# Two transformer layers on one core: copies of transposed chunks by ScalarE alone, or by whichever of VectorE and ScalarE is free

## The chip, the cores and the metric

The kernel runs on 1 core of one Trainium2 chip. A core has TensorE (PE in the profile, its weight loads PEld), VectorE (DVE), ScalarE (ACT), GpSimd (POOL) and SyncE (SP), each with its own queue of instructions that it works through in order, and DMA queues that move data between HBM and the on-chip memory SBUF. Matmul results land in PSUM, a small memory that VectorE and ScalarE read. The metric is the device time of one execution in microseconds (us).

## The reference

Input x is 2 x 1024 tokens of width 512, all in fp32. Two layers follow each other, each of two parts, and every part ends in `x = layernorm(x + part(x))`:

```
q, k, v = silu(x Wq), silu(x Wk), silu(x Wv)              # 16 heads of 32
S_t = exp(ld) S_(t-1) + k_t v_t^T ;  o_t = q_t S_t         # linear attention with decay
o = rmsnorm_per_head(o * sigmoid((x Wg1) Wg2)) * w ; part = o Wo
part = fwht(silu(x W1^T) * (x W3^T)) W2^T                  # fwht: Hadamard transform over 2048
dt_r, B, C = split(x Wbc^T) ; delta = softplus(dt_r Wdt^T + b_dt)
h_t = exp(delta_t A) h_(t-1) + (delta_t x_t) B_t ; part = sum_n h_t[n] C_t[n] + x D   # scan, 32 states
part = (silu(x Wg^T) * (x Wu^T)) Wd^T
```

The first two lines with S are layer 0's attention, then layer 0's feed-forward net; the scan is layer 1's mixer, and the last line layer 1's net.

## The kernel before

**Tiling.** Tokens are cut into chunks of 128 (the partitions of SBUF) and chunks into five groups, `GROUPS`: group 0 has the first 2 chunks of sequence 0, group 1 the first 4 of sequence 1, group 2 the next 4 of sequence 0, group 3 the last 4 of sequence 1, group 4 the last 2 of sequence 0. A chunk of x lies as tokens x 512 columns in a tile `xn`. A matmul over the 512 columns needs them on the partitions, so the chunk is transposed first.

**Phases.** Each group passes through `V` (values of the attention, L607), `A` (the rest of the attention, `L658` its projections of q and k, L845 scores, L891 and L900 outputs, L1003 the product with Wo), `F` (layer 0's net: L1052 gate and up products, L1106 the product with Wd), the scan, and `f` (layer 1's net, same lines). `PHASES` gives the order in which phases take PE: V0 A0 V1 A1 F0 F1 V2 A2 f0 F2 V3 A3 a1 F3 V4 A4 b1 F4 f2 f3 f4. Here a1 and b1 are the two halves of f1. F0, f0, a1 and b1 are fillers: they run at a lower priority in the gaps of the attention of another group, and read the tile `xf` instead of `xT`.

**Turning a chunk.** `turn(dst, gi, c, stage)` transposes chunk c of group gi four times 128x128 on PE (L527) into one PSUM bank of the pool `mm` (four banks), and a small thread `copied` copies the bank into its columns of the tile `xT` or `xf` (L534). It is called for every chunk four times: stage 0 for V, 1 after the attention for F, 2 for the scan's inputs, 3 after the scan for f. That makes 64 copies of 128x512, all on ScalarE.

**The scan's inputs.** `Scan.inputs` turns the group's chunks (stage 2), starts `residual` for each (L1284 on POOL), multiplies all of them by Wbc (L1252, which needs the last copy), copies the result (L1258, ScalarE), and multiplies by Wdt (L1269); four softplus chains on ScalarE (L1303 to L1313) and products on POOL (L1322, L1330) follow. The scan itself is POOL's products (L1390), ScalarE's exponentials (L1410), VectorE's scans (L1438) and products (L1451), and sums on POOL and by accumulating DMAs (L1487, L299); VectorE's last column of a unit is kept by ScalarE (L1463). `outputs` transposes the sums back on PE (L1516), and VectorE adds them to the chunk (L1531).

**Normalization.** `normalized` is three small instructions on VectorE (L556 to L558) and four on ScalarE (L562 to L565) for each chunk. ScalarE uses several tables of functions; a change of table is an ACT_TABLE_LOAD.

**The order.** All work is written as generators that yield `Op`s. The class `Order` runs them against its own model of the five engines before anything is built: `free[engine]` is the time at which the model has the engine free, `begin` when an op's operands and buffers are there, `us` its modelled duration. For each engine the best op is taken: of those that could start when the engine becomes free, the one of the lowest `prio` (and, after that, the one that needs no other table), otherwise the one that can start first; among the engines the one whose op starts earliest goes next. The order in which ops are put is the order of each engine's queue on the chip, where semaphores make an instruction wait for its operands. A copy of a transposed chunk has prio -1, a normalization between parts -2, scans and their products 1. The model's constants are in the class (`HOP`, `QUEUE`, and so on).

The pool `mm` holds 4 PSUM banks for nearly all of PE's results. VectorE has one other stream before the first scan: the Hadamard transform of W2 (butterflies L1167, then products L1186 on PE).

Of the kernel before, what the change touches and what calls it, by code (L numbers as in the profile page):

```python
# [53 lines left out]
class Buf:  # L54


    def __init__(self, refs=1):
        self.t = None
        self.written = None
        self.last = 0.0  # L60
        self.refs = refs
# [6 lines left out]
class Op:  # L68

    def __init__(self, eng, us, fn, r=(), w=(), a=(), free=(), prio=0, table=None, dma=0,
                 spare=0):
        self.eng, self.us, self.fn, self.prio, self.table, self.dma = eng, us, fn, prio, table, dma
        self.r, self.w, self.a, self.free, self.spare = r, w, a, free, spare


class Order:
# [4 lines left out]


    ENGINES = ("PE", "DVE", "ACT", "POOL", "SP")
    HOP = 0.08
    QUEUE = 220e3
    FIRST, ALONE = 350e3, 30.0

    def __init__(self):
        self.free = {e: 0.0 for e in self.ENGINES}
        self.queue = {e: 0.0 for e in self.ENGINES}
        self.tags = {}
# [8 lines left out]
    def spawn(self, gen, prio=0):  # L103
        self.new.append([gen, prio, None])

    def begin(self, op, spare=True):

        t = self.free[op.eng]
        for b in op.r:
            if b.written is None:  # L110
                return None
            t = max(t, b.written + self.HOP)
        for b in op.w:
            t = max(t, b.last + self.HOP)
        for name in {name for name, _ in op.a}:
            n, _, bufs = self.tags[name]
            k = sum(name == v for v, _ in op.a) + (op.spare if spare else 0) - (n - len(bufs))
            if k > 0:
                free = sorted(b.last for b in bufs if b.refs <= 0)
                if len(free) < k:  # L120
                    return None
                t = max(t, free[k - 1] + self.HOP)
        return t
# [42 lines left out]
    def run(self):  # L166
        while True:
            while self.new:
                th = self.new.pop(0)
                if self.advance(th):  # L170
                    self.threads.append(th)
            best = {}
            last = None
            moved = False
            for th in list(self.threads):
                op = th[2]
                if not isinstance(op, Op):
                    if op():
                        moved = True
                        if not self.advance(th):  # L180
                            self.threads.remove(th)
                    continue
                t = self.begin(op)
                if op.spare:
                    t0 = self.begin(op, False)
                    if t0 is not None and (last is None or t0 < last[1]):
                        last = None, t0, th
                if t is None:
                    continue
                prio = op.prio + th[1]  # L190
                wrong = self.switches(op)
                now = t <= self.free[op.eng]
                key = (0, prio, wrong, t) if now else (1, t, prio, wrong)
                if op.eng not in best or key < best[op.eng][0]:
                    best[op.eng] = (key, t, th)
            if moved or self.new:
                continue

            if last and ("PE" not in best or best["PE"][1] > last[1] + 1.0):
                best["PE"] = last  # L200
            if not best:
                assert not self.threads, [
                    (th[0].__name__, getattr(th[2], "eng", None)) for th in self.threads
                ]
                return
            _, t, th = min(best.values(), key=lambda v: v[1])
            self.put(th[2], t)
            if not self.advance(th):
                self.threads.remove(th)
# [3 lines left out]
def two_layers(  # L213
# [5 lines left out]
    nc = tc.nc  # L219
# [63 lines left out]
    def pe(us, fn, **kw):  # L283
        return Op("PE", us, fn, **kw)
# [235 lines left out]
    def turn(dst, gi, c, stage, prio=-1):  # L520

        bank = Buf()
        at = dst.cs.index(c)

        def transposes():
            for db in range(EB):
                nc.tensor.transpose(  # L527
                    bank.t[:, db * P : (db + 1) * P],
                    xn[gi, c].t[:, db * P : (db + 1) * P], ident,
                )  # L530

        def copied():
            yield Op(
                "ACT", 0.68, lambda: nc.scalar.copy(  # L534
                    dst.t[:, :, at * P : (at + 1) * P],
                    bank.t.rearrange("p (k t) -> p k t", t=P),
                ),
                r=[bank, dst.whole], w=[dst.parts[at]], free=[bank], prio=-1,
            )

        yield pe(0.62, transposes, r=[xn[gi, c], there[gi, c, stage], ident_b],
                 a=[("mm", bank)] + ([] if at else [(dst.tag, dst.whole)]), prio=prio)
        spawn(copied())
# [1114 lines left out]
```

## Time and profile before

| | us |
|---|---|
| median of 3 runs | 1821.92 (1817.36 to 1825.52) |
| profiled execution | 1821.05 |
| its span | 1819.3 |
| PE busy | 1769.7 |
| VectorE busy | 1283.0 |
| ScalarE busy | 1160.8 |
| GpSimd busy | 1097.2 |
| mean granted TensorE clock | 0.987 |

The times of the profile are of one execution, counted from the start of its span. Lines of an instruction read: start, duration, engine, line, operation, output <- input, shape, how many, and in brackets how long the engine was idle before it and whose end released it. Several instructions of a kind in a row are merged into one line. Lines of waits read: who waited <- for whom, us in total, times, the longest. `ACT_TABLE_LOAD` is a change of ScalarE's table. fp32 matmuls of the program show as two in the profile, so that a product over the 512 columns is eight.

Around the 64 copies, from the groups of instructions: 56 into `xT` take 586 ns each and 8 into `xf` 587. VectorE's operations on 512 columns out of PSUM take about 0.68 us (L1083 679 ns, L1125 680 ns, L1017 685 ns).

### The profile page before, as it was taken

The numbers are of one execution on the slowest core, as the hardware profiler recorded it, in microseconds if no ns is written. First come the engines' busy times: TensorE is split into PE (matmuls) and PEld (weight loads), VectorE is DVE, ScalarE is ACT, GpSimd is POOL, SyncE is SP. The second block draws the span as 40 slices with busy tenths as digits, with TensorE's granted clock in tenths as the row PEclk, the third lists the DMA queues.
The fourth block names the chain that finished last, engine by engine and source line by source line (L and its number), as shares of the span: only waits on it lengthen the run. The fifth ranks groups of instructions, "written<-read, shape, count | busy, mean of one in ns | idle before, by whom it ended". The sixth has DMA issues, their size and how long they took to land.

```text
span 1819.3 us, 21238 instructions
## 1 busy us (share of the span) xinstructions
PE 1769.7 (97%) x7064; PEld 1001.4 (55%) x7064; DVE 1283.0 (71%) x1537; ACT 1160.8 (64%) x1830; POOL 1097.2 (60%) x595
## 2 busy tenths in 40 slices
PE   7999999998899999999999999999999999999998
PEld 4556764443466744444666444576865444544574
DVE  4643114988399889952999999539999899998211
ACT  3634237688876776768767768686766868775311
POOL 2000004977577979934779899438998998676000
PEclk8999999999999999999999999999999999999999
DMA  9533435666558868844678788467989875766251
GB/s 278 160 112 97 149 126 166 180 184 177 179 153 230 231 182 237 217 116 147 186 209 232 198 239 217 142 203 245 271 241 263 205 209 162 194 177 168 81 173 58
DMA packets 225420, 336.32 MB, mean 185 GB/s; under 512 B 19568, under 2 KB 128896, under 8 KB 225312
## 3 DMA queue, kind: packets, MB, share of 16 engines
q1 hardware_dynamic: 206192, 270.86, 46.9%
q0 software_dynamic: 16816, 59.92, 17.5%
q10 hardware_dynamic: 2304, 4.20, 0.6%
q8 instruction: 56, 0.92, 0.2%
q14 instruction: 52, 0.43, 0.1%
HBM read 253.12 MB, written 22.54 MB: 152 GB/s over the span
## 4 chain that ended last, share of the span: by engine, by line
PE 69%; DVE 12%; ACT 9%; issue 4%; DMA 3%; POOL 2%; SPq 0%; DVEq 0%; POOLq 0%; ACTq 0%
PE mm L1052 38%; PE mm L1106 18%; DVE da L1438 6%; PE mm L658 3%; ACT da L1410 2%; PE mm L1003 2%; DVE dbu L1451 2%; PE mm L607 2%; DMA y<-dbu 1%; ACT L501 1%; POOL dbu L1390 1%; ACT L1410 1%; PE mm L845 1%; PE mm L527 1%; ACT L498 1%
## 5 line engine op out<-in xcount | busy, mean ns | idle before, releaser
L1390 POOL TENSOR_TENSOR dbu<-du,B 128x1024 f32<-128x1024 f32 x256 | 653.0, 2576 | 123.0 <-DMA y<-dbu 90.9
L1052 PE MATMUL mm<-xT,w 128*128 128x512 f32 (+1 forms) x1912 | 667.6, 509 | 2.5 <-ACT h L501 1.7
L1052 PEld LDWEIGHTS mm<-xT,w 128*128 128x128 f32 x1912 | 363.0, 190 | 303.6 <-issue 266.0
L1410 ACT ACTIVATE da<-delta,a_s 128x512 f32<-128x512 f32 (+1 forms) x640 | 384.4, 605 | 150.3 <-DVE dbu L1451 119.6
L1438 DVE TENSOR_TENSOR_SCAN da<-da,hlast,dbu 128x512 f32<-128x512 f32 (+1 forms) x384 | 425.7, 1109 | 35.9 <-ACT da L1410 23.1
L1487 POOL TENSOR_TENSOR y<-y,dbu 128x1024 f32<-128x1024 f32 x123 | 325.6, 2647 | 50.7 <-DVE dbu L1451 47.9
L1106 PE MATMUL mm<-w,h 128*128 128x512 f32 x768 | 339.1, 595 | 2.5 <-DMA w<-w2h 1.9
L1451 DVE TENSOR_TENSOR dbu<-da,C 128x1024 f32<-128x1024 f32 x256 | 312.8, 1222 | 13.2 <-ACT hlast L1463 6.4
L1438 DVE TENSOR_TENSOR_SCAN da<-da,dbu 128x256 f32<-128x256 f32 (+1 forms) x256 | 246.0, 961 | 25.4 <-ACT da L1410 18.5
L1106 PEld LDWEIGHTS mm<-w,h 128*128 128x128 f32 x768 | 145.1, 191 | 176.1 <-issue 165.2
L1052 PE MATMUL mm<-xf,w 128*128 128x256 f32 x1024 | 228.6, 382 | 0.8 <-ACT sg L778 0.8
L1052 PEld LDWEIGHTS mm<-xf,w 128*128 128x128 f32 x1024 | 194.2, 191 | 32.9 <-issue 4.4
L501 ACT ACT_TABLE_LOAD x142 | 182.2, 1283 | 6.8 <-PE mm L658 3.5
L501 ACT ACTIVATE h<-mm 128x512 f32<-128x512 f32 x144 | 85.8, 597 | 119.8 <-PE mm L1052 68.7
L1083 DVE TENSOR_TENSOR h<-h,mm 128x512 f32<-128x512 f32 x96 | 65.2, 679 | 111.0 <-PE mm L1052 97.6
L1410 ACT ACT_TABLE_LOAD x109 | 139.8, 1283 | 1.9
L658 PE MATMUL mm<-xT,w 128*128 128x512 f32 (+1 forms) x320 | 120.5, 526 | 4.8 <-DVE sc L863 1.4
L299 POOL DMA_DIRECT2D y<-dbu x113 | 111.3, 985 | 15.7 <-DVE dbu L1451 7.3
L748 POOL TENSOR_TENSOR qd<-h,q_dec 128x512 f32<-128x512 f32 x14 | 18.2, 1297 | 164.4 <-ACT h L501 102.8
L1463 ACT COPY hlast<-da 128x2 f32<-128x2 f32 (+1 forms) x160 | 25.4, 159 | 139.6 <-DVE dbu L1451 119.1
L1106 PE MATMUL mm<-w,hf 128*128 128x512 f32 x256 | 112.8, 592 | 0.0
L1125 DVE TENSOR_TENSOR xn<-mm,xn 128x512 f32<-128x512 f32 x60 | 40.8, 680 | 93.9 <-PE mm L1106 93.7
(100 smaller groups left out, 1356.8 us busy)
## 6 DMA issues: line engine op xcount, KB each, us to landing
y<-dbu POOLq DMA_DIRECT2D x113, 512.0 KB, 6.1
w<-in_wgut_dram SPq DMA_DIRECT2D x192, 256.0 KB, 4.6
B<-rows SPq DMA_DIRECT2D x128, 256.0 KB, 4.5
C<-rows SPq DMA_DIRECT2D x128, 256.0 KB, 4.2
w<-in_wdnt_dram SPq DMA_DIRECT2D x96, 256.0 KB, 4.8
w<-in_w1t_dram SPq DMA_DIRECT2D x80, 256.0 KB, 4.7
w<-in_w3t_dram SPq DMA_DIRECT2D x80, 256.0 KB, 5.1
w<-w2h SPq DMA_DIRECT2D x80, 256.0 KB, 4.2
```

Source lines behind the costliest of these rows:

```text
L299: return Op(eng, us, lambda: of.dma_start(dst(), src(), **more), dma=nbytes, **kw)
L501: nc.scalar.activation(dst, src, AF.Silu)
L658: nc.tensor.matmul(bank.t[:, s * T : (s + 1) * T], w_qk[j][k].t[:, eb * P : (eb + 1) * P], xT.t[:, k, :], start=k == 0, stop=k == EB - 1,)
L1052: nc.tensor.matmul(bank.t[:, s * T + c0 * P : s * T + c1 * P], blocks[fb // 2][j][k // 2].t[:, k % 2 * 2 * P + k0 : k % 2 * 2 * P + k0 + P ...
L1083: 512, lambda: nc.vector.tensor_mul(t.t, t.t, pu.t), r=[pu], w=[t], free=[pu]
L1106: nc.tensor.matmul(accs[c].t, hT[f // S].t[:, s * T + c * P : s * T + (c + 1) * P], w_d[f].t, start=f == 0, stop=f == nt * S - 1,)
L1125: nc.vector.tensor_add(xb.t, bank.t, xb.t)
L1390: 1024, lambda: nc.gpsimd.tensor_mul(self.wide(self.db[i]), self.wide(du), self.row(self.bs, i)),
L1410: nc.scalar.activation(d[:, j, :], self.wide(delta)[:, j, :], AF.Exp, scale=a_s[:, k0 + j, n : n + 1],)
L1438: nc.vector.tensor_tensor_scan(d()[:, j, :], d()[:, j, :], self.wide(db)[:, j, :], init, ALU.mult, ALU.add,)
L1451: 1024, lambda: nc.vector.tensor_mul(self.wide(db), d(), self.row(self.cs, i)),
L1487: 1024, lambda: nc.gpsimd.tensor_add(y.t, y.t, db[i].t), r=o, w=[y],
```

## The change

An `Op` can now carry a second way to run: another engine, duration and function. Each time the planner looks at such an op it takes the first way, unless the second way's engine is free in the model more than `MARGIN` = 1.0 us before the first's. Only the copies of transposed chunks get a second way: the same copy by VectorE, with the same modelled duration of 0.68. Nothing else in the program is edited, but as the planner decides everything in turn, later ops can come in another order too.

```diff
@@ class Op @@
     def __init__(self, eng, us, fn, r=(), w=(), a=(), free=(), prio=0, table=None, dma=0,
-                 spare=0):
+                 spare=0, other=None):
+        self.ways = [(eng, us, fn), other] if other else None
         self.eng, self.us, self.fn, self.prio, self.table, self.dma = eng, us, fn, prio, table, dma
@@ class Order @@
     ENGINES = ("PE", "DVE", "ACT", "POOL", "SP")
+    MARGIN = 1.0
...
             for th in list(self.threads):
                 op = th[2]
+                if isinstance(op, Op) and op.ways:
+                    first, second = op.ways
+                    op.eng, op.us, op.fn = first
+                    if self.free[second[0]] + self.MARGIN < self.free[first[0]]:
+                        op.eng, op.us, op.fn = second
                 if not isinstance(op, Op):
@@ turn @@
         def copied():
-            yield Op(
-                "ACT", 0.68, lambda: nc.scalar.copy(
+            def ends_of():
+                return (
                     dst.t[:, :, at * P : (at + 1) * P],
                     bank.t.rearrange("p (k t) -> p k t", t=P),
-                ),
+                )
+
+            yield Op(
+                "ACT", 0.68, lambda: nc.scalar.copy(*ends_of()),
                 r=[bank, dst.whole], w=[dst.parts[at]], free=[bank], prio=-1,
+                other=("DVE", 0.68, lambda: nc.vector.tensor_copy(*ends_of())),
             )
```

In the order that is built so, 15 of the 64 copies stand on VectorE. By group and chunk: (0,1) and (1,3) of stage 0; (1,2) and (1,3) of stage 1; (0,1) of stage 2; (2,2) and (2,3) of stage 0; (2,2) and (2,3) of stage 2; (1,0) and (1,1) of stage 3, into `xf`; (3,2) and (3,3) of stage 2; (4,1) of stage 1; (4,1) of stage 2.

## The prediction

> **What bounds the kernel now.** I read the page's busy shares first, then what PE (TensorE) waited for, then the instructions around its longest waits, and last the granted clock there.
>
> ```profile
> PE 1769.7 (97%) x7064; PEld 1001.4 (55%) x7064; DVE 1283.0 (71%) x1537; ACT 1160.8 (64%) x1830; POOL 1097.2 (60%) x595
> PE 69%; DVE 12%; ACT 9%; issue 4%; DMA 3%; POOL 2%; SPq 0%; DVEq 0%; POOLq 0%; ACTq 0%
> ...
> PE mm L1252 <- ACT xT L534: 6.6, 2, 3.6
> PE mm L1186 <- issue: 4.6, 1, 4.6
> PE mm L527 <- DMA xn<-in_x_dram: 4.1, 1, 4.1
> PE mm L527 <- DVE h L1083: 2.0, 1, 2.0
> PE mm L1516 <- ACT h L501: 2.0, 1, 2.0
> ```
>
> PE is busy 1769.7 of 1819.3 us, so it is idle 49.6 us, and its last matmul ends some 6 us before the span does. Whatever the change does to ScalarE or VectorE counts only through those 49.6 us, or by adding to them. Moving copies can shorten waits that a copy ended; the only large ones are the two at L1252 (3.6 and 3.0 us), the first product of the scan's inputs, which needs the last transposed chunk of its group. The second of them, in time:
>
> ```profile
> 803.85 0.63 PE L527 MATMUL mm<-cst,xn 128*128 128x128 f32 x4
> 804.32 3.60 PE L607 MATMUL mm<-w,xT 128*128 128x512 f32 x8
> 807.75 1.40 PE L527 MATMUL mm<-cst,xn 128*128 128x128 f32 x8
> 812.16 6.50 PE L1252 MATMUL mm<-xT,wbc 128*128 128x512 f32 x8 [3.00 <-ACT xT L534]
> ...
> 808.78 0.15 DVE L558 TENSOR_SCALAR neg<-mv 128x1 f32<-128x1 f32 x1
> ...
> 810.82 0.81 ACT L565 ACTIVATE xn<-xn,nmr,rstd 128x512 f32<-128x512 f32 x1
> 811.54 0.56 ACT L534 COPY xT<-mm 128x512 f32<-128x512 f32 x1
> 812.00 1.07 ACT L534 COPY xf<-mm 128x512 f32<-128x512 f32 x2
> 813.08 1.28 ACT L501 ACT_TABLE_LOAD   x1
> ```
>
> The chunk was transposed by 804.48, but ScalarE copied it at 811.54, after four normalizations (L562 to L565). VectorE was done at 808.93. PE stood still for 3.00 us, and then its eight products took 6.50 us where eight of that shape take 3.43 (L607: 804.32 to the next start at 807.75). The clock says why (columns: window, its length, busy us of PE, PEld, DVE, ACT, POOL, PEclk, DMA share, GB/s):
>
> ```profile
> 806.00:809.00 3.00, 2.85 (x13) 1.49 (x11) 2.80 (x8) 2.80 (x9) 0.00 (x0) 1.00 0.74 236
> 809.00:812.00 3.00, 0.15 (x2) 0.00 (x0) 0.00 (x0) 2.87 (x7) 0.00 (x0) 0.83 0.63 201
> 812.00:815.50 3.50, 3.34 (x4) 1.51 (x5) 0.00 (x0) 2.96 (x5) 0.00 (x0) 0.50 0.00 0
> 815.50:819.00 3.50, 3.50 (x7) 1.47 (x6) 0.00 (x0) 0.31 (x1) 0.00 (x0) 0.67 0.00 0
> 819.00:822.00 3.00, 3.00 (x8) 1.06 (x6) 0.00 (x0) 0.27 (x1) 0.00 (x0) 1.00 0.20 44
> ```
>
> So this place costs 3.00 us idle and 3.07 us at half clock.
>
> **What moves.** In the built order of the changed kernel 15 of the 64 copies stand on VectorE; 49 stay. PE's order is 99% the same: 36 of its 3,726 instructions as the program lists them change place. I take the copies by place.
>
> *Price of one.* On ScalarE a copy takes 0.585 us (L534, 64 of them), so ScalarE loses 15 x 0.585 = 8.8 us. No such copy runs on VectorE before; a 128x32 copy takes 0.186 there (L813), a 512-column operation out of PSUM 0.68 (L1083, L1125, L1017), the costliest such 0.74 (L952). I take 0.68, the row of the same size and source: VectorE gains 10.2 us. [...]
>
> *Scan inputs of group 2, chunks (2,2) and (2,3), and the two copies to xf after them.* Three of these copies now follow VectorE's last moments, ending at 808.93. The copy that L1252 needs ends there at 808.93 + 0.68 = 809.6, PE's transposes end at 809.15, L1252 can start at about 809.7: the wait falls from 3.00 to 0.55, which is -2.45. If the clock isn't lowered after so short a gap, its products take 3.43: another -3.07. Gaps of 2.02 us (L527 at 1124.74, the eight products after it 5.09) and 3.61 (L1252 at 442.74, 5.18) were followed by a lowered clock; after the 1.67 at 1427.45 eleven products took 4.99 us, near 11 x 0.43 = 4.7. So 0.55 should not. What is late next: L1269 needs ScalarE's copy of L1252's result. ScalarE ends its norms at 811.63, then a table load and a silu (1.28 + 0.60) to 813.5, the copy (0.58) to 814.1; PE comes to L1269 after L1252 and eight products of L658, 809.7 + 3.43 + 3.43 = 816.6. Covered by 2.5 us. Sum of the place: **-5.5**. VectorE and POOL have nothing to do from 812 to 819 (0.00 in the rows), so all later work moves forward with PE.
>
> [...] The row shows a lowering after 3.00 idle and a loss of 3.07; the sum goes by the row.
>
> *Startup, chunk (0,1).* L607 waits for its weights at 7.82 (1.50 on the DMA), 0.9 us past the copy's end: 0.
>
> *(1,3) for V1, at 61.10.* VectorE takes it between two butterfly steps (L1167) and must wait for the transposes until 61.0: its chain slips by up to 1.4 + 0.68. The butterfly that ends at 68.97 is read at 71.53: cover 2.5 us. 0, at most +0.5.
>
> *(1,2), (1,3) into F1, near 186.* VectorE is busy 7.9 of 60 us from 200 to 260, and PE has other products first: 0.
>
> *Scan inputs of group 0, (0,1), at 258.14.* Its L1252 now comes one product (1.72 us) earlier, at 259.4; VectorE, idle from 254.8, ends the copy by 258.7. PE's work only changes order: 0.
>
> *(2,2), (2,3) for V2, at 406 and 417.* VectorE adds L1125 just before (404.30 to 404.97), so the copy ends no later than ScalarE's: 0. The first L1252 wait (442.74) has its copy still on ScalarE, behind the same instructions: its 3.6 us stay.
>
> *Group 3, (3,2), (3,3), near 1155 to 1176.* L1252 starts at 1176.38 without a wait: 0.
>
> *Group 4, (4,1) into F4 and for its scan.* The second transposes now follow three gate/up products, not four, so they come 1.7 us earlier, and must find a chunk normalized at 1390.38. VectorE does that group's add one scan (1.29) earlier, which makes the chunk ready at about 1389. Between -0.46 (the wait of L1052 on L1125 at 1386.23 goes) and, if copy or norm come late, a gap like the one at 442.74, 3.61 + (5.18 - 3.43) = +5.4. I take 0: VectorE's order puts the copy behind two scans that end near 1391, and PE needs it near 1391.6.
>
> *The output of scan 3, at 1520.* Two products (6.9 us) move from behind its transposes (L1516) to before them; behind them stand 6.9 us of L1106. L1516 waited 1.96 + 0.94 there for banks and the products after it took 8.04 instead of 6.9: down to -4.0 if all that goes. The last chunk was normalized 8.6 us after L1516's end, so up to +1.5 if the shorter cover fails. I take 0, the middle being near and the sign open.
>
> **Sum.** 1821.05 (profiled execution: span 1819.3 and 1.75 around it; the median of the runs is 1821.92) - 5.5 = **1815.6 us**. All bounds together: 1821.05 - 5.5 - 0.5 - 4.0 = 1811, and, if the group-2 place gains nothing, 1821.05 + 0.5 + 5.4 + 1.5 = 1828.5.
>
> **Rivals.**
> - *The gap shrinks, the clock falls anyway* (or falls elsewhere, since its drops sit at many places): 1821.05 - 2.45 = 1818.6. For it: losses of 1.7 to 3.1 us after gaps of 2.0 to 3.6 don't follow the length of the gap. Against: no drop after short gaps.
> - *The wait only changes its name*: VectorE serves the copy no sooner, or L1269 waits instead: 1821, or up to 1826 with group 4's gap. For it: VectorE's queue is as strict in its order as ScalarE's. Against: 2.5 us of cover.
> - *More is gained at 1520*: 1821.05 - 5.5 - 4.0 = 1811.6.
> - *Slower: VectorE becomes the bound.* From 1000 to 1150 it is busy 142.4 of 150 us, and a copy queued there also waits for its transposes with the scans behind it. If all 15 copies fall on the path: 1821.05 + 15 x 0.68 = 1831.3. It decides where more than 5.5 / 0.68 = 8 copies stand in scan stretches with PE waiting for the scan. Against it: only four do (two near 410, two near 1390), and in the list of PE's waits none ends on a scan (L1438), its product (L1451) or a sum on POOL.
>
> **How the numbers follow.** Main case 0.45, clock falls anyway 0.18, renamed wait 0.17, more at 1520 0.12, VectorE the bound 0.08. The runs before spread from 1817.36 to 1825.52, so about 0.5% (9.1 us) is what a measurement can tell from no change: below 1812.8 and above 1831.0. Faster: most of the 1811.6 case and the lower edge of the main case, 0.19. Slower: half of the VectorE case and a tail of the renamed wait, 0.09. Same: 0.72. The range runs from 1808 (the 1811.6 case less the spread of a median) to 1827 (the renamed wait with a gap), which leaves out the VectorE case and the tails.
>
> **What the next profile would show.** Right: L534's successor with 15 copies on DVE near 0.68 us and 49 on ACT; one wait of some 3.6 us at the scan's first product, and none over 1 us at the one near 810; there a clock of 1.00 and eight products in 3.4 to 3.6 us; PE busy within a few us of 1767, idle near 47. Wrong: a clock drop there although the gap is short; a new gap of PE over 2 us near 1390 or 1525; or VectorE copies that run longer than 0.74 us.

## The result, and the profile after

The changed kernel takes 1824.58 us (median of 21 runs, 1820.30 to 1827.14); beside it the kernel before took 1821.34 (21 runs, 1812.69 to 1825.76). The ratio is 1.0025, 95% interval 1.0015 to 1.0034: 3 to 6 us slower, where 5.5 us faster was forecast. It lies inside the forecast range and inside the half per cent that was called "same", but on the wrong side.

The page of the kernel after: busy us of each engine, and the chain that ended last. Then PE's longest waits (us in total, times, longest), behind two that both kernels have: for the first load of x (4.1 us before, 4.8 after) and at the products with the transformed W2 (4.6 and 4.5).

```profile
PE 1772.3 (97%) x7064; PEld 1005.4 (55%) x7064; DVE 1292.1 (71%) x1552; ACT 1154.0 (63%) x1815; POOL 1097.1 (60%) x595
PE 77%; DVE 7%; ACT 6%; DMA 6%; POOL 2%; issue 2%; SPq 0%; DVEq 0%; ACTq 0%; POOLq 0%
```

```profile
...
PE mm L1264 <- ACT xT L548: 3.6, 1, 3.6
PE mm L1528 <- ACT h L509: 3.6, 1, 3.6
PE mm L1118 <- DVE h L1095: 2.5, 1, 2.5
PE mm L1064 <- ACT h L509: 2.2, 1, 2.2
```

Lines of the kernel after stand 8 to 12 lower: L1264 is the scan inputs' first product (L1252 before), L548 and L550 are the copy on ScalarE and on VectorE, L509 is the silu of the gate (L501), L1095 its product with the up half (L1083), L1528 the transposes of the scan's output (L1516), L1118 and L1064 the down and the gate/up products (L1106 and L1052).

The wait of 3.00 us at L1252 is gone and the 3.6 us one stays, both as forecast. Three waits of 2.2 to 3.6 us are new. PE is busy 2.6 us longer than before, where about 2.7 less was forecast.

The place near 812 us in time, kernel after (L535 are the transposes, L527 before, and L670 the products with the weights of q and k, L658 before):

```profile
809.80 1.40 PE L535 MATMUL mm<-cst,xn 128*128 128x128 f32 x8
811.64 3.70 PE L1264 MATMUL mm<-xT,wbc 128*128 128x512 f32 x8 [0.44 <-DVE xT L550]
815.18 3.60 PE L670 MATMUL mm<-xT,w 128*128 128x512 f32 x8
...
810.91 0.68 DVE L550 COPY xT<-mm 128x512 f32<-128x512 f32 x1
```

and its clock (start:end, length, busy us of PE, PEld, DVE, ACT, POOL, granted clock, DMA share, GB/s):

```profile
812.00:815.50 3.50, 3.50 (x9) 1.52 (x8) 0.78 (x2) 3.37 (x8) 0.00 (x0) 1.00 0.29 101
```

PE waits 0.44 us, its eight products take 3.70 instead of 6.50, and the clock is 1.00 instead of 0.50.

To see where the time went, I matched PE's instructions of the two traces one to one and took the difference of their starts (after less before). It is a ledger of two single executions:

| stretch | difference at its start, us | at its end, us | what lies there |
|---|---|---|---|
| 0 to 54 us | 0 | +1.16 | the first load of x lands 0.69 us later, then scatter |
| 470 to 805 | +0.46 | +2.04 | the clock, at 0.50 from 483.31 to 490.14 and 500.38 to 503.80 before, from 481.37 to 491.61 and 512.09 to 515.50 after (-1.7 to +1.7 each); a wait of 1.07 at 510 |
| 812 to 818 | +2.04 | -3.31 | the place above: -5.35 (forecast -5.5) |
| 885 to 892 | -3.30 | -1.80 | the clock falls (0.50 from 884.14 to 887.55) at gaps of 1.21 and 0.69 us that both kernels have |
| 1378 to 1542 | -2.04 | +4.17 | group 4: +6.21 |
| 1701 to the end | +3.67 | +3.6 | |

In this pair of executions the forecast gain came to within 0.15 us. The stretch in which I had priced everything at nothing took 6.2 us. PE's waits there, kernel after:

```profile
1416.39 24.30 PE L1064 MATMUL mm<-xT,w 128*128 128x512 f32 x56 [0.80 <-ACT pt L1315]
1449.20 21.73 PE L1118 MATMUL mm<-w,h 128*128 128x512 f32 x50 [2.49 <-DVE h L1095]
1521.19 8.83 PE L1064 MATMUL mm<-xT,w 128*128 128x512 f32 x16 [2.21 <-ACT h L509]
1534.46 0.66 PE L1528 MATMUL mm<-cst,y 128*128 128x128 f32 x4 [3.56 <-ACT h L509]
```

Before, the longest of this stretch were 1.96 and 1.67 us. All of PE's waits in it make 9.35 us, against 5.40 before; most of the rest of the 6.2 us is the clock, which is lowered for 3.41 us twice there (from 1522.43 and from 1536.08), and once before. ScalarE's rows behind the two last waits:

```profile
1505.76 0.60 ACT L509 ACTIVATE h<-mm 128x512 f32<-128x512 f32 x1
1513.14 1.28 ACT L1422 ACT_TABLE_LOAD   x1 [6.78 <-DMA delta<-dd]
...
1519.25 1.28 ACT L509 ACT_TABLE_LOAD   x1
1520.54 0.60 ACT L509 ACTIVATE h<-mm 128x512 f32<-128x512 f32 x1
```

ScalarE stands 6.78 us in front of an exponential of group 4's scan, whose input delta has not landed. The silu that PE waits for is queued behind it, and comes 14.8 us after the one before. Why delta is late shows on SyncE's queue. The kernel before, then the kernel after:

```profile
1500.02 0.33 SPq L299 DMA_DIRECT2D du<-dd  x1
1500.43 0.40 SPq L299 DMA_DIRECT2D delta<-dd  x1
```

```profile
1501.96 0.33 SPq L307 DMA_DIRECT2D du<-dd  x1
1502.38 2.63 SPq L307 DMA_DIRECT2D w<-in_wdnt_dram  x4
1505.10 0.87 SPq L307 DMA_DIRECT2D delta<-dd  x1
```

The planner's new order put four weight loads between the two. Delta's load is issued 4.7 us later than before, and takes 8.0 us where it took 4.3.

### The profile page after: what moved, and what is told of

The parts are those of the page before. It is cut to its first block, busy times and chain, and to the rows that moved or that the text cites. A ratio compares the mean times of both kernels' runs of the same rounds, so it can differ in the third digit from the quotient of the medians.

```text
span 1822.9 us, 21229 instructions
## 1 busy us (share of the span) xinstructions
PE 1772.3 (97%) x7064; PEld 1005.4 (55%) x7064; DVE 1292.1 (71%) x1552; ACT 1154.0 (63%) x1815; POOL 1097.1 (60%) x595
## 4 chain that ended last, share of the span: by engine, by line
PE 77%; DVE 7%; ACT 6%; DMA 6%; POOL 2%; issue 2%; SPq 0%; DVEq 0%; ACTq 0%; POOLq 0%
PE mm L1064 42%; PE mm L1118 21%; PE mm L670 4%; DVE da L1450 3%; DMA y<-dbu 2%; PE mm L1015 2%; PE mm L619 2%; POOL dbu L1402 1%; DVE dbu L1463 1%; PE mm L535 1%; PE mm L857 1%; ACT da L1422 1%; ACT L506 1%; ACT L509 1%; DMA w<-in_wq_dram 1%
## 5 line engine op out<-in xcount | busy, mean ns | idle before, releaser
L1064 PE MATMUL mm<-xT,w 128*128 128x512 f32 (+1 forms) x1912 | 668.1, 510 | 3.4 <-ACT h L509 2.2
L1064 PEld LDWEIGHTS mm<-xT,w 128*128 128x128 f32 x1912 | 363.7, 191 | 306.3 <-issue 268.6
L1118 PE MATMUL mm<-w,h 128*128 128x512 f32 x768 | 340.5, 597 | 4.9 <-DVE h L1095 2.5
L1118 PEld LDWEIGHTS mm<-w,h 128*128 128x128 f32 x768 | 145.9, 192 | 179.6 <-issue 167.4
L1064 PE MATMUL mm<-xf,w 128*128 128x256 f32 x1024 | 229.7, 383 | 0.8 <-ACT sg L790 0.8
L1064 PEld LDWEIGHTS mm<-xf,w 128*128 128x128 f32 x1024 | 195.6, 192 | 33.5 <-issue 4.7
L509 ACT ACTIVATE h<-mm 128x512 f32<-128x512 f32 x144 | 85.8, 597 | 123.7 <-PE mm L1064 70.0
L1095 DVE TENSOR_TENSOR h<-h,mm 128x512 f32<-128x512 f32 x96 | 65.1, 678 | 101.0 <-PE mm L1064 99.3
L670 PE MATMUL mm<-xT,w 128*128 128x512 f32 (+1 forms) x320 | 119.3, 522 | 4.8 <-DVE sc L875 1.4
L1118 PE MATMUL mm<-w,hf 128*128 128x512 f32 x256 | 112.8, 592 | 0.0
```

The lines of the kernel that those rows point to most:

```text
L509: nc.scalar.activation(dst, src, AF.Silu)
L670: nc.tensor.matmul(bank.t[:, s * T : (s + 1) * T], w_qk[j][k].t[:, eb * P : (eb + 1) * P], xT.t[:, k, :], start=k == 0, stop=k == EB - 1,)
L1064: nc.tensor.matmul(bank.t[:, s * T + c0 * P : s * T + c1 * P], blocks[fb // 2][j][k // 2].t[:, k % 2 * 2 * P + k0 : k % 2 * 2 * P + k0 + P ...
L1095: 512, lambda: nc.vector.tensor_mul(t.t, t.t, pu.t), r=[pu], w=[t], free=[pu]
L1118: nc.tensor.matmul(accs[c].t, hT[f // S].t[:, s * T + c * P : s * T + (c + 1) * P], w_d[f].t, start=f == 0, stop=f == nt * S - 1,)
```

## The experiments

All ratios are to the kernel before, run beside each; us are the ratio's distance from 1 times 1820.

**Group 2's copies alone.** Only the copies of group 2's scan inputs and those to xf behind them may move; (2,2), (2,3) and the two to xf do. The order of PE, POOL and SyncE is that of before.

```
-other=("DVE", 0.68, ...tensor_copy...),
+other=("DVE", 0.68, ...tensor_copy...) if (gi, stage) in ((2, 2), (1, 3)) else None,
```

> Only the copies of group 2's scan inputs, (2,2) and (2,3), and the two copies to xf after them may go to VectorE; PE's order is that of before. Theory A (the gain at group 2's place is real, the loss of the change lies at group 4): the wait of about 3.0 us at the scan inputs' first product falls to about 0.5 us, the eight products take about 3.7 us instead of 6.5, and the time is 4 to 5.5 us below before, a ratio near 0.9973. Rival B (the gain is given back later whatever is done at group 4, by a clock drop or a wait elsewhere): 0 to -2.5 us, a ratio from 0.9987 to 1.0000. Rival C (copies on VectorE cost the path by themselves): slower than before.

Measured: 0.9995 (0.9983 to 1.0008), -0.9 us. Rival B's size, not theory A's. In the trace the place itself gains 5.36 us on PE, but 2.7 of them are given back from 880 to 892 us and 1.4 from 1184 to 1221. The first of these, in this run (the gaps, then the clock):

```profile
880.32 1.59 PE L857 MATMUL mm<-h 32*128 32x128 f32 x16 [1.21 <-DVE xT L931]
882.17 2.07 PE L948 MATMUL mm<-sg,cst 128*128 128x512 f32 x2 [0.25 <-ACT sg L938]
884.03 5.44 PE L1064 MATMUL mm<-xf,w 128*128 128x256 f32 x16
```

```profile
880.00:885.00 5.00, 4.43 (x21) 2.92 (x22) 4.98 (x7) 3.51 (x6) 4.92 (x3) 0.59 0.02 5
```

and in the kernel before, where the gaps are 1.21 and 0.69 us:

```profile
887.78 1.13 PE L936 MATMUL mm<-sg,cst 128*128 128x512 f32 x2 [0.69 <-ACT sg L926]
888.75 3.62 PE L1052 MATMUL mm<-xf,w 128*128 128x256 f32 x16
```

```profile
885.00:890.00 5.00, 3.38 (x24) 2.58 (x25) 5.00 (x8) 2.91 (x5) 4.92 (x3) 1.00 0.07 24
```

The same sixteen products take 3.62 us there and 5.44 here. Whether such a fall belongs to the kernel or to the execution is looked at below.

**The change without group 4's copies.**

```
+other=... if gi < 4 else None,
```

> The change with group 4's copies left on ScalarE: 13 copies still move, PE's order after 800 us is that of before. Theory A (all of the loss comes from group 4's new order): as the run of group 2 alone, 4 to 5.5 us below before, 7 to 10 us below the changed kernel. Rival C (each copy on VectorE costs some of its 0.68 us): as the changed kernel or worse, 13/15 of its loss. Rival D (the loss comes from the other 9 moved copies of groups 0, 1 and 3): slower than the run of group 2 alone by more than 2 us.

Measured: 0.9985 (0.9972 to 0.9997), -2.7 us; 7.3 us below the changed kernel (1.0025). The loss is bound to group 4. Rivals C and D fall: with nine more copies on VectorE than the run before, the time is no higher. Here too 1.5 us go at 885 (clock 0.79 and 0.87).

**Group 4's copies alone.**

```
+other=... if gi == 4 else None,
```

> Only group 4's copies may go to VectorE (two of chunk (4,1) do): until about 1380 us the order is that of before, from there on that of the changed kernel. Theory A: the gain at 812 us is missing and the loss at 1440 to 1540 us stands alone: 7 to 10 us above before, a ratio near 1.0045. Rival B (the loss arises wherever time was gained earlier, not from the order): within 1 us of before. In the trace theory A wants PE's waits of about 2.5 us near 1450 and of 2.2 and 3.6 us near 1520 to 1535, with ScalarE standing about 6 us on the load of delta.

Measured: 1.0046 (1.0030 to 1.0062), +8.4 us, as theory A had it. Two copies of 64 make the whole loss. The order is new earlier than I had expected: the first of the two copies, (4,1) for F4, stands at 1244.3 us in the kernel before, and from about 1240 us on VectorE, ScalarE, POOL and SyncE work in another order; PE's differs from 1390 on. The traces' rows are those of the changed kernel: ScalarE stands 6.99 us for delta, PE waits 2.39 us near 1449 and 4.42 near 1534. The parts add up: -2.7 and +8.4 make +5.7, inside the changed kernel's +2.7 to +6.2.

**Delta's load behind du's.** The changed kernel, with group 4's two loads issued as one step, so that nothing stands between them.

```
+if self.gi == 4:
+    both = ((self.du, 1), (self.delta, 0))
+    yield Op("SP", 0.12, lambda: [
+        nc.sync.dma_start(self.wide(of[kp]), self.dd[r, :, k2, :]) for of, r in both], ...)
+    return
```

> The changed kernel, but group 4's loads of du and delta are issued one directly behind the other, so that no weight load stands between them in SyncE's queue. Theory A1 (ScalarE's stand of 6.78 us on the load of delta makes the waits at 1520 to 1535 us): the stand falls below 3 us, PE's waits of 2.2 and 3.6 us there fall by 3 us together or more, and the time falls by 3 to 5 us against the changed kernel, to a ratio of 0.9995 to 1.0010 against before. Rival A2 (the silus are late for another reason, the stand only fills time in which ScalarE had nothing else ready): the time is within 1 us of the changed kernel, ratio about 1.0025.

Measured: 1.0003 (0.9989 to 1.0017), +0.5 us: 4.0 us (about 3 either way) off the changed kernel's loss. Theory A1 holds in time; in the rows it holds in part:

```profile
1507.43 1.28 ACT L1433 ACT_TABLE_LOAD   x1 [3.74 <-DMA delta<-dd]
...
1527.34 1.10 PE L1539 MATMUL mm<-cst,y 128*128 128x128 f32 x4 [3.01 <-ACT h L509]
1528.94 1.11 PE L1539 MATMUL mm<-cst,y 128*128 128x128 f32 x4 [0.51 <-DVE h L1095]
```

The stand falls from 6.78 to 3.74 us, not below 3, and PE's waits there from 6.1 us (2.21, 3.56 and 0.29) to 3.5. The wait of 2.4 us near 1447 is untouched. This run too is ordered anew behind its edit, on SyncE from 1502 us on and on PE from 1546, so that the 4.0 us are not shown to be the load's alone.

**And every second softplus of group 4 with a buffer of its own**, against ScalarE's stand of 3.36 us on POOL near 1441, which I took for the cause of the wait at 1449.

```
-a=[("th", a)]
+a=[("sc" if self.gi == 4 and k % 2 else "th", a)]
```

> The kernel of the run before with one edit more: every second softplus chunk of group 4 has a tile of its own in place of the one buffer that ScalarE shares with POOL there, so ScalarE's stand of about 3.3 us on POOL near 1441 us should go. Theory A (both stands of ScalarE cause the loss): PE's wait of 2.4 to 2.5 us near 1447 falls below 1 us, and the time falls by another 2 to 4 us, to a ratio of 0.9985 to 0.9993 against before, like the change without group 4's copies. Rival A2 (the silu behind the stand is late for another reason, or the waits come back near 1525 us): within 1 us of the run with the delta load alone, a ratio of 1.0000 to 1.0006.

Measured: 1.0041 (1.0027 to 1.0054), +7.5 us. Both expectations were wrong. The stand on POOL is gone, and PE waits near 1450 all the same; worse, a wait of 6 us has come up later:

```profile
1441.55 6.28 PE L1118 MATMUL mm<-w,h 128*128 128x512 f32 x14 [0.95 <-ACT h L509]
1450.05 21.73 PE L1118 MATMUL mm<-w,h 128*128 128x512 f32 x50 [2.23 <-DVE h L1095]
1530.44 1.12 PE L1539 MATMUL mm<-cst,y 128*128 128x128 f32 x4 [6.05 <-DVE h L1095]
1534.40 1.12 PE L1539 MATMUL mm<-cst,y 128*128 128x128 f32 x4 [2.84 <-DVE xn L1554]
```

This time the silu near 1446 is done at 1446.02, and it is its product on VectorE that comes at 1449.32, behind a product and a scan. Near 1510 to 1523 VectorE stands 5.30 and 2.83 us for POOL. No single stand is shown to make group 4's loss, and the softplus buffer isn't shown to be a cause by itself: taking one wait out, and letting the planner order the rest anew, put another in its place.

**Two scan chunks by decree.** Only (1,3) and (2,3) for the scan go to VectorE, whatever the model's free times say; these are the copies behind the waits of 3.61 and 3.00 us.

```
+other=... if (gi, c, stage) in ((1, 3, 2), (2, 3, 2)) else None, margin=-1e9,
-if self.free[second[0]] + self.MARGIN < self.free[first[0]]:
+if self.free[second[0]] + op.margin < self.free[first[0]]:
```

> Only the last chunk of the scan inputs of group 1 and that of group 2, (1,3) and (2,3), go to VectorE, both by decree and not by the model's free times: the two copies on which PE waits for 3.61 and 3.00 us in the kernel before. Theory A (a copy on VectorE is worth what it takes off PE's wait): the place near 812 us gains 5 us as in the run of group 2 alone; the place near 443 us gains up to 3.6 + 1.7 = 5.3 us, less about 1.5 to 2.5 us since VectorE has scans and products queued there (2.9 and 1.2 us long): in all 6 to 9 us, less what a clock drop gives back, a ratio from 0.9950 to 0.9980. Rival C (the planner's new order after 440 us costs as group 4's did): slower than the run of group 2 alone, a ratio from 0.9995 to 1.0050.

Measured: 0.9923 (0.9911 to 0.9935), -14.0 us, more than any theory allowed. This beats both kernels. The wait near 443 is only renamed: eight products of L672 now come first, and then PE waits for another copy of ScalarE's.

```profile
452.75 5.04 PE L1283 MATMUL mm<-pt,wdt 64*128 64x512 f32 x6 [2.80 <-ACT pt L1272]
```

But the planner, given this copy, orders the work from there on anew, and waits elsewhere go: by the ledger, 4.5 us from 390 to 607, 2.2 at 680 (the wait of 1.92 us for a load of w2h) and 7.7 from 682 to 818. The next runs take this apart.

**All 64 copies on VectorE**, the same way.

> All 64 copies on VectorE by decree. Rival C (VectorE becomes the bound, every copy costs its 0.68 us of the end): 64 x 0.68 = +43.5 us, a ratio near 1.024. Theory A (only where VectorE's queue is full of scans while PE needs the chunk does a copy cost): the startup and the groups' first stages cost nothing, perhaps 8 to 16 copies in scan stretches cost 1 to 3 us each: +8 to +30 us, a ratio from 1.004 to 1.016. Under both PE's waits should name the copy on VectorE.

Measured: 1.0037 (1.0024 to 1.0050), +6.7 us: a tenth of a microsecond for a copy of 0.68. VectorE as the bound falls; theory A's lower end (+8) is just above. The longest wait of PE that names a copy is 0.8 us; the longest of all are for other work in a new order (7.3 us for kd, 5.1 for h).

**Group 2 alone, once more, for its profile.**

> The kernel of the run of group 2 alone, once more, for its profile. In that run PE gained 5.36 us near 812 us and gave 2.7 us of it back near 880 to 890 us, where after gaps of 1.21 and 0.25 us the clock fell to 0.59, while the kernel before kept 1.00 there after 1.21 and 0.69. Theory P (the fall is bound to where the gap lies in time or to what went before, and so to the kernel): the same fall at the same place, 1.4 to 2.7 us lost from 880 to 890. Rival R (it is chance of one execution): no fall there, and the gain of 5.3 us lasts past 890.

Measured, in one execution of 1815.88 us: the fall is there again, clock 0.71 and 0.61 from 880 to 890 us, 2.9 us given back. That spoke for theory P, but other runs speak against it. Four runs have the same order of all engines up to about 1240 us, so up to there they are the same work: the kernel before, group 4's copies alone, and the two runs that follow. The gaps of 1.21 and 0.69 us are in all four; the clock stays at 1.00 in the first two and falls in the last two (0.85 from 885 to 890 us, 0.60 from 891 to 895). So with this order it is the execution and not the kernel that decides, as rival R has it, and two equal outcomes for one kernel prove nothing. (What differs between the executions stands in the last section.) The same four show the wait of 3.00 us at group 2's scan inputs, and the eight products behind it take 6.50, 5.40, 3.70 and 5.20 us. The third of them (group 4's order alone):

```profile
815.38 3.70 PE L1264 MATMUL mm<-xT,wbc 128*128 128x512 f32 x8 [3.00 <-ACT xT L548]
```

and the last (group 4's engine alone):

```profile
817.07 5.20 PE L1266 MATMUL mm<-xT,wbc 128*128 128x512 f32 x8 [3.00 <-ACT xT L548]
```

By these four the clock behind that wait costs 1.5 us on the mean (5.20 less 3.70); the profiled execution of the kernel before was the dearest of them.

**Group 4: the order alone.** The two copies are planned for VectorE and issued on ScalarE.

```
-other=("DVE", 0.68, lambda: nc.vector.tensor_copy(*ends_of())),
+other=("DVE", 0.68, lambda: nc.scalar.copy(*ends_of())) if gi == 4 else None,
```

> Group 4's two copies are planned for VectorE as in the run with group 4's copies alone, but issued on ScalarE: PE, POOL and SyncE have the same order as in that run, only the two copies stand on the other engine. Theory A (what costs is the planner's new order of group 4, not the engine of the copies): the loss of that run stays, +6 to +11 us against before, a ratio from 1.003 to 1.006. Rival E (the copies cost by standing in VectorE's queue between scans): the loss goes, within 2 us of before.

**Group 4: the engine alone.** Planned for ScalarE, with no second way for any copy, and the two issued on VectorE.

```
+"ACT", 0.68, lambda: (nc.vector.tensor_copy if (gi, c) == (4, 1) and stage in (1, 2)
+                      else nc.scalar.copy)(*ends_of()),
```

> The converse: group 4's two copies are planned for ScalarE, so that every engine's order is that of before, but issued on VectorE. Theory A: within 2 us of before, a ratio from 0.9990 to 1.0010, and PE's waits near 1450, 1520 and 1535 us as in the kernel before. Rival E: +4 to +11 us.

Measured: the order alone 1.0062 (1.0045 to 1.0079), +11.3 us; the engine alone 0.9998 (0.9983 to 1.0014), -0.4 us. This is the clearest pair of the study. The orders of PE, POOL and SyncE are those of the run with group 4's copies alone in the first, and those of before in the second. With both copies on ScalarE the new order costs all of the loss and perhaps a little more; with both copies on VectorE and the old order nothing is lost. PE's waits say the same, the order alone first:

```profile
1454.84 23.42 PE L1118 MATMUL mm<-w,h 128*128 128x512 f32 x50 [2.69 <-DVE h L1095]
1540.33 2.06 PE L1528 MATMUL mm<-cst,y 128*128 128x128 f32 x8 [4.42 <-ACT h L509]
```

```profile
1432.86 17.43 PE L1066 MATMUL mm<-xT,w 128*128 128x512 f32 x40 [2.33 <-ACT h L509]
1528.66 0.66 PE L1530 MATMUL mm<-cst,y 128*128 128x128 f32 x4 [1.96 <-ACT h L509]
1530.25 1.12 PE L1530 MATMUL mm<-cst,y 128*128 128x128 f32 x4 [0.94 <-DVE h L1097]
```

The second list has the waits of the kernel before at the same places (1.67, 1.96 and 0.94 us there; only the first is longer here, 2.33).

**The run with two scan chunks, with (2,3) back on ScalarE.** All orders stay.

```
-if (gi, c, stage) in ((1, 3, 2), (2, 3, 2))
+if (gi, c, stage) in ((1, 3, 2),)
```

> The run with two scan chunks on VectorE, which was 14 us faster than before, with the copy of (2,3) back on ScalarE: all orders are the same, this copy alone has changed its engine. Theory A (each of the two waits is worth its idle time and the clock drop behind it, 5.4 us near 812): 5 us slower than that run, 9 us faster than before, a ratio of 0.9945 to 0.9955, with PE's wait near 800 us back at about 3 us. Rival F (the new order after 440 us brings most of the gain): within 2 us of the run with both, a ratio from 0.992 to 0.993.

Measured: 0.9935 (0.9919 to 0.9952), -11.8 us. The time alone would leave both theories open, but the trace decides for F:

```profile
795.13 0.60 PE L536 MATMUL mm<-cst,xn 128*128 128x128 f32 x4
795.56 3.60 PE L621 MATMUL mm<-w,xT 128*128 128x512 f32 x8
799.00 1.91 PE L1530 MATMUL mm<-cst,y 128*128 128x128 f32 x16
800.75 3.60 PE L1266 MATMUL mm<-xT,wbc 128*128 128x512 f32 x8
```

The wait of 3.00 us at group 2's scan inputs is gone with the copy on ScalarE. In this order ScalarE copies the chunk at 796.64, before the four other normalizations (801.78 to 808.31) that stood in front of it in the kernel before, and PE has 5.2 us of other products between the transposes and the first product that needs it.

**The same two chunks, the engine alone.** Planned for ScalarE, with no second way, and issued on VectorE.

```
+"ACT", 0.68, lambda: (nc.vector.tensor_copy if (gi, c, stage) in ((1, 3, 2), (2, 3, 2))
+                      else nc.scalar.copy)(*ends_of()),
```

> The same two copies, (1,3) and (2,3) for the scan, issued on VectorE, but planned for ScalarE: every engine's order is that of before. Theory A (the copies' place behind fewer instructions is what gains): the wait near 812 us falls from 3.0 to about 0.5 us and the one near 443 us from 3.6 to 1 to 2 us, 5 to 9 us faster than before, a ratio from 0.9950 to 0.9975. Rival F (the planner's new order brings the rest): about -1 to -3 us as the run of group 2 alone, so that 10 us or more of the 14 come from the order.

Measured: 0.9981 (0.9971 to 0.9992), -3.5 us, nearer to rival F: some 10 of the 14 us are the order's, though that order with both copies on ScalarE was not run. The two places:

```profile
442.06 5.20 PE L1266 MATMUL mm<-xT,wbc 128*128 128x512 f32 x8 [3.29 <-DVE xT L548]
811.02 3.70 PE L1266 MATMUL mm<-xT,wbc 128*128 128x512 f32 x8 [0.45 <-DVE xT L548]
```

At 811 the wait falls as forecast. At 442 it changes its name and loses 0.32 us: VectorE comes to the copy behind scans, as ScalarE came to it behind a normalization, a silu and exponentials.

The study in one table. "Order" is that of all work other than the moved copies; the numbers in it are places in the kernel, in us.

| run | copies moved | order | us against before (95%) |
|---|---|---|---|
| the change | 15 | new from 260 to 430 and from 1240 | +4.5 (+2.7 to +6.2) |
| group 2 alone | 4 | old | -0.9 (-3.1 to +1.5) |
| without group 4 | 13 | new from 260 to 430 | -2.7 (-5.1 to -0.5) |
| group 4 alone | 2 | new from 1240 | +8.4 (+5.5 to +11.3) |
| the change, delta's load behind du's | 16 | as the change, anew from 1500 | +0.5 (-2.0 to +3.1) |
| the same, softplus buffer too | 16 | as the run above, anew from 1410 | +7.5 (+4.9 to +9.8) |
| group 4, planned for VectorE, run on ScalarE | 0 | as group 4 alone | +11.3 (+8.2 to +14.4) |
| group 4, planned for ScalarE, run on VectorE | 2 | old | -0.4 (-3.1 to +2.5) |
| two scan chunks by decree | 2 | new from 440 | -14.0 (-16.2 to -11.8) |
| one of them | 1 | the same new one | -11.8 (-14.7 to -8.7) |
| two scan chunks, planned for ScalarE | 2 | old | -3.5 (-5.3 to -1.5) |
| all 64 | 64 | new | +6.7 (+4.4 to +9.1) |

## Why the prediction was right and wrong

- *Price of a copy: right.* 13 copies to xT at 685 ns and two to xf at 679 on VectorE, 49 left at 587 and 586 on ScalarE; 0.68 and 0.585 were used. That the sum holds nothing for VectorE's 10.2 us was right too: with 13 copies moved and group 4's left the time is 2.7 us below before.
- *Group 2's place: the wait right, the clock's term mis-sized.* The wait fell to 0.44 (0.55 forecast), the clock to 1.00, and the ledger has -5.35 where -5.5 was forecast. But the term of -3.07 for the clock takes 3.43, from the first start to the next product's, off 6.50, which runs to the last end; alike by alike (6.50 less 3.60) it is 2.90, and the place -5.35. And it was read from one execution: over four the term is 1.5, and the place is worth 2.56 + 1.5 = 4.1. The runs that hold this gain in the old order of that place measured -0.9, -2.7 and -3.5 us, 2.4 on the mean. What lies between 2.4 and 4.1 is within their intervals, and isn't explained further.
- *"Against: no drop after short gaps": wrong.* The clock falls at gaps of 1.21 and 0.69 us near 885, in some executions (to 0.50 from 884.14 in the kernel after). The kernel before's own trace, in rows that I hadn't weighed, said so: eight products took 6.00 us at 485.48, with the clock at 0.50 from 483.31 on, behind gaps of 0.78 and 0.67, and 5.40 behind a gap of 1.06 (499.82). The rival "the clock falls elsewhere" was closer than its 0.18. With the old order a fall at 885 came in some executions without the change too, so it isn't shown to be the change's doing.
- *The step that failed: "Group 4, (4,1) into F4 and for its scan ... I take 0", and with it "the output of scan 3, at 1520 ... I take 0".* I priced the first as a local matter of whether the copy comes in time at 1390, and took no account of the other one, for F4, at 1244. In time it is: PE has no wait from 1380 to 1400, and even loses the 0.46 us it had. What I left out is that the planner built everything behind the two copies anew: SyncE's loads, POOL's products, ScalarE's exponentials and silus, VectorE's scans. That cost 6.2 us on PE in the ledger, and +8.4 us alone; with the order of before the same two copies on VectorE cost nothing (-0.4). The bounds for the second place (-4.0 to +1.5) came from PE's own order there, and looked at no other queue. About 4 us of the loss went in the run that undid one row of SyncE's queue, delta's load behind four weight loads; as that run also changed the order behind, the row's own share is not shown. The other 3 to 4 us belong to the same order, but to no single stand that I could name, and taking away the one that I tried (the softplus buffer) brought another wait. Which rows of the new order make the loss stays open in this measure.
- *The 3.6 us at 443 stay: right,* and the reason too: with the copy on VectorE in the old order the wait is 3.29.
- *The rivals.* "VectorE the bound" is out: all 64 copies cost 6.7 us, not 43.5. "The wait only changes its name" did not happen at 812; it is what happens at 443. The upper case in it, 1826 with a gap of group 4's, has the right size and the right group, but the gap was placed at 1390, and the cause was not a late copy.
- *Signs to look for.* A new gap of PE over 2 us near 1525 was listed as what would show the forecast wrong, and that is what the profile has. PE's busy time was to fall to about 1767 us and its idle time to 47; they are 1772.3 and 50.6.

## What to carry to other kernels

Where a planner orders the queues, an edit of one step's engine is an edit of all that it plans afterwards: planning and issuing apart (the same orders with the step on either engine, and the new orders with the step on the old one) tells the two effects from each other in two runs, and here the engine was worth 0 to -3.5 us and the order -10 to +11. Before pricing such an edit by its own place, compare the built orders of every queue behind it, the DMA queues first, and ask for each moved load which engine stands in order behind its data. Here a load that was issued beside its pair and then came behind four others went with some 4 us, and no moved pair of copies was worth more than 3.5 by its engine.

## What the runs showed of the hardware that was not expected

- *The same gap, with and without a lowered clock.* Behind the same wait of 3.00 us in the same order, eight products took 3.70, 5.20, 5.40 and 6.50 us in four executions; behind gaps of 1.21 and 0.69 us two of them kept the clock at 1.00 and two lost it (0.85 from 885 to 890 us, 0.60 from 891 to 895). The traces show what differs. In those of the kernels before and after, every one of the 9 and 10 lowered stretches, at 0.50, lasts 3.41 us, or two, three or four times that (the last of each trace is cut short by the end), and within a trace all of them lie on one grid of 3.41 us, which lies differently in each execution: a step begins at 810.99 us before, at 812.46 after. Two executions cut along their grids, the kernel before (6.50 us) and group 4's order alone (3.70):

```profile
807.58:810.99 3.41, 1.43 (x9) 0.78 (x7) 1.25 (x5) 3.18 (x10) 0.00 (x0) 1.00 0.92 290
810.99:814.40 3.41, 2.24 (x3) 1.18 (x4) 0.00 (x0) 3.39 (x6) 0.00 (x0) 0.50 0.04 14
```

```profile
810.03:813.45 3.42, 2.20 (x11) 1.11 (x9) 1.99 (x7) 3.22 (x10) 0.00 (x0) 1.00 0.97 308
813.45:816.86 3.41, 1.48 (x4) 0.77 (x5) 0.00 (x0) 3.31 (x7) 0.00 (x0) 1.00 0.20 71
```

In the first the wait leaves PE 1.43 us of work in one step of the grid, and the next two steps are lowered. In the second the grid divides the wait between two steps, with 2.20 and 1.48 us of work, and nothing is lowered. Where the products took 5.40 and 5.20 us, the wait leaves 0.74 and 0.66 us in one step, and one step is lowered. Near 885 us it is alike: both gaps lie in one step in the two executions that lost the clock (1.51 and 1.55 us of work left), and in two steps in the two that kept it (2.21 and 2.72; 2.47 and 2.45). How much work keeps the clock isn't shown: 1.48 us did, 1.55 did not, nor did 2.20 in the run of group 2 alone (the step before 880.88) or 2.45 in the kernel before (the step before 483.31). So the loss behind such a wait is none, one or two steps, here 0, 1.5 to 1.7 or 2.8 us, and a clock loss read from one trace is one draw. Its place in the forecast is a range.
- *A load's time.* Delta's 512 KB took 4.3 us from issue to landing directly behind du in the kernel before, 8.0 us behind du and four weight loads, and 6.9 us directly behind du in the run that undid this. So giving it back its place in the queue took back 1.1 of the 3.7 us; where the rest comes from is not shown.
